# Sums over edges: strips cut by edges instead of by nodes, and a matmul that takes a node tile out of them

## The chip, the cores and the metric

One core of one Trainium2 chip runs the kernel. The metric is the device time in microseconds of one execution, as the median of several runs. One further execution was recorded by the hardware profiler; everything said of engines and waits comes from that one.

## The reference

The input is a matrix x of 6250 nodes by 512 features and a list of 100,000 edges (src, dst), sorted by dst; all is f32. With LN(v) = (v - mean) / sqrt(variance + 1e-5) over a row:

```
h0 = LN(x)
for layer in 1, 2:
    agg[n] = sum of h[src] over the edges whose dst is n
    deg[n] = number of those edges
    h = relu(h @ W_self + (agg / max(deg, 1)) @ W_neigh + b)
x = x + h
f = LN(x)
per node: the two of 8 experts with the largest f @ Wg, weights by softmax
    y_e = LN(relu(f @ W1[e] + b1[e]) @ W2[e] + b2[e]) * gamma[e] + beta[e]
x = x + weighted sum of the two y_e
```

All weight matrices are 512 by 512, except Wg (512 by 8).

## The kernel before

A **node tile** is 128 nodes: 49 of them. An **edge tile** is 128 edges: the rows h[src] of its edges, 128 by 512 f32 (256 KB), are fetched from memory by one indirect load on the POOL queue (a **gather**, L272). They are summed by dst on TensorE: a one-hot matrix `hot` (edges by nodes) is the stationary operand and the gathered rows the moving one, so that the output row of a node is the sum of its edges' rows.

The program has five stretches.

*Norms and edge tables.* x comes in twelve loads (`xt`) on the SP queue, is normed, turned, and written to `xn_d` in memory; the gathers of layer 1 read `xn_d`. For the first 19 node tiles (NS) the product with W_self of layer 1 is made here already and kept in `big` (`part(b)`); for the others the turned rows are kept there. Between the second and the third `xt` load, `edge_tables` makes two tables in the on-chip buffer: `srcT`, the indices of each gather, and `rel`, the dst of each edge relative to its group. A **group** is 256 nodes (25 groups). Since the edges of a group begin at any edge, a chain of operations counts the edges below each group (last edges of blocks of 1000, a comparison, a matmul, an indirect load, a comparison, a sum), and 50 loads on the SP queue then start at offsets read from registers.

*Layer 1* (`sums` with `layer1`). Each group is taken as having T = 34 edge tiles (15 in the last), more than it needs on average, so that nearly any draw fits: 831 gathers. A group's nodes are cut into eight **strips** of 32 nodes. Which edge tiles a strip can touch is not known when the program is built, so a span wide enough by 4.5 standard deviations is used: an edge tile is multiplied with every strip that it might touch (1.8 on average, 1513 strip matmuls per layer). A strip matmul has a stationary operand of 128 by 32 and occupies one of four column quarters of the array (`tile_position`); the quarters of 128 nodes fill the 128 partitions of one accumulator bank, `pa0` or `pa1` (one bank each). The order of edge tiles in a group alternates between its two ends, so that neighbours in the order fall into different quarters.

The order on TensorE, VectorE, ScalarE and POOL is written out by hand (`manual_schedule`): a loop over **slots** of four edge tiles. In slot i the program issues the gathers of slot i+2 into a ring of 12 row buffers, builds the `hot` matrices that fall due, adds two edge tiles, does the items due in the place "mid", adds two more, calls `finish` for a node tile whose last strip is complete, and does the items due in the place "post". `finish` for layer 1 (`layer1`) makes the degree from a sum of the hot matrices (`hs`, L292, `few`, L448, and a matmul `pn`, L449), scales the sum into `a` on ScalarE, and leaves items for the next slots: u0 (product of the own rows with W_self, only from tile 19 on, which opens an accumulator `pm`), u1 (turn `a`, L241 and L243), u2 (product with W_neigh, added to u0's accumulator, and one add, L427), u3 (turn), u4 and u5 (products with the two matrices of layer 2, written to memory as `z2` and `s2`). All products are in `project` (L413), four matmuls each; `pm` has three banks.

A check between the layers compares the sum of all degrees with the number of edges; where they differ, an unlimited but slow loop over all edges (`slow_path`) runs at the end.

*Layer 2* (`sums` with `route`). The neighbour product was applied before the sum, so the gathers read `z2`. `route` adds, norms, and chooses the experts of a tile over the next slots (`turn`, `logits`, `experts`, `rank`, two `send` on the POOL queue that scatter the rows into `xs` by expert, `share`, and at six points `take`, which makes the table of expert tiles known so far). In every second slot in which the table holds one, an **up-projection** (`Up`: load, turn, product `ph` at L734, turn, store) of an expert tile runs between the sums; there are 68 of them. Rows go through a ring of 12 parts of `big`. The last sends each wait for the send before.

*Experts.* 105 expert tiles are finished (the rest of the up-projections, the down-projections at L995, norm, store), the eight scatters of zero rows at the experts' ends each waiting for the one before, and the results are gathered per node and added.

Of the kernel before, what the change touches and what calls it, by code (L numbers as in the profile page):

```python
# [29 lines left out]
F32 = mybir.dt.float32  # L30
# [9 lines left out]
P = 128  # L40
SW = 32
NQ = P // SW
GN = 2 * P
# [4 lines left out]
RW = 1000  # L48
# [7 lines left out]
class Group:  # L56


    def __init__(self, g, N, E):
        self.g = g  # L60
        self.nodes = min(GN, N - g * GN)
        per = E / N
        self.T = ceil((self.nodes * per + 4 * sqrt(self.nodes * per)) / P)
        ns = ceil(self.nodes / SW)
        self.span = []
        for q in range(ns):
            a, z = q * SW * per, min((q + 1) * SW, self.nodes) * per
            lo = max(0, floor((a - 4.5 * sqrt(a)) / P))
            hi = min(self.T - 1, floor((z + 4.5 * sqrt(z)) / P))
            self.span.append((lo, self.T - 1 if q == ns - 1 else hi))  # L70
        self.nt = ceil(self.nodes / P)

        self.order = []
        cut = (self.T * P // GN) - 1 if self.nt == 2 else self.T
        for a, z in ((0, cut), (cut, self.T)):
            h = (z - a + 1) // 2
            for i in range(h):
                self.order += [t for t in (a + i, a + h + i) if t < z]
        self.strips = {t: [q for q, (lo, hi) in enumerate(self.span) if lo <= t <= hi] for t in self.order}
        self.first = {q: next(t for t in self.order if q in self.strips[t]) for q in range(ns)}  # L80
        self.last = {q: [t for t in self.order if q in self.strips[t]][-1] for q in range(ns)}

        self.done = [max(self.order.index(self.last[q]) for q in range(ns) if q // NQ == k)
                     for k in range(self.nt)]
        self.ns = ns
# [3 lines left out]
def gnn_moe(ctx, tc, x, src, dst, Ws1, Wn1, gb1, Ws2, Wn2, gb2, Wg, W1, b1, W2, b2, gamma, beta, out):  # L89
# [10 lines left out]
    groups = [Group(g, N, E) for g in range((N + GN - 1) // GN)]  # L100
    NG = len(groups)
    T = groups[0].T
    GB = P // T
    col = [g.g * T for g in groups]
    NCOL = col[-1] + groups[-1].T
    EP = E + T * P
    assert D == 512 and H == 512 and NE == 8 and E % RW == 0 and E // RW <= P

# [4 lines left out]
    dpad = dram.tile([EP], I32, name="dpad")  # L113
    spad = dram.tile([EP], I32, name="spad")

# [10 lines left out]
    iota_row = iota([P, GN], "iota_row", [[1, GN]])  # L126
# [14 lines left out]
    rel = edges.tile([P, NCOL], F32, name="rel")  # L141
    srcT = edges.tile([P, NCOL], I32, name="srcT")


    def edge_tables():
        with tc.tile_pool(name="prep", bufs=1, side="right") as prep, \
                tc.tile_pool(name="prep_r", bufs=3, side="right") as raw, \
                tc.tile_pool(name="prep_ps", bufs=1, space=PSUM) as pps:
            nrow = E // RW
            dst_r = dst.rearrange("(r e) -> r e", e=RW)  # L150
            last_i = prep.tile([nrow, 1], I32, name="last_i")
            nc.scalar.dma_start(last_i, dst_r[:, RW - 1 : RW])
            pad = prep.tile([T, P], I32, name="pad")
            nc.gpsimd.memset(pad, -1)
            pad0 = prep.tile([T, P], I32, name="pad0")
            nc.gpsimd.memset(pad0, 0)
            nc.scalar.dma_start(dpad[:E], dst)
            nc.scalar.dma_start(dpad[E:].rearrange("(t e) -> t e", e=P), pad)
            nc.scalar.dma_start(spad[:E], src)
            nc.scalar.dma_start(spad[E:].rearrange("(t e) -> t e", e=P), pad0)  # L160
            last = prep.tile([nrow, 1], F32, name="last")
            nc.vector.tensor_copy(last, last_i)
            thr = prep.tile([P, NG], F32, name="thr")
            nc.vector.tensor_scalar(thr, iota_row[:, :NG], float(GN), None, op0=OP.mult)
            thr_p = prep.tile([P, 1], F32, name="thr_p")
            nc.vector.tensor_scalar(thr_p, iota_p, float(GN), None, op0=OP.mult)
            below = prep.tile([nrow, NG], F32, name="below")
            nc.vector.tensor_scalar(below, thr[:nrow], last, None, op0=OP.is_gt)
            pr = pps.tile([NG, NDEG], F32, name="pr")
            nc.tensor.matmul(pr, below, ones[:nrow, :NDEG], start=True, stop=True)  # L170
            row = prep.tile([NG, 1], F32, name="row")
            nc.vector.tensor_scalar(row, pr[:, 0:1], float(nrow - 1), None, op0=OP.min)
            row_i = prep.tile([NG, 1], I32, name="row_i")
            nc.vector.tensor_copy(row_i, row)
            at_i = prep.tile([NG, RW], I32, name="at_i")
            nc.gpsimd.indirect_dma_start(
                out=at_i, out_offset=None, in_=dst_r,
                in_offset=bass.IndirectOffsetOnAxis(ap=row_i[:, 0:1], axis=0))
            at = prep.tile([NG, RW], F32, name="at")
            nc.vector.tensor_copy(at, at_i)  # L180
            nc.vector.tensor_scalar(at, at, thr_p[:NG], None, op0=OP.is_lt)
            cnt = prep.tile([NG, 1], F32, name="cnt")
            nc.vector.tensor_reduce(cnt, at, AX.X, OP.add)
            start = prep.tile([NG, 1], F32, name="start")
            nc.vector.scalar_tensor_tensor(start, row, float(RW), cnt, op0=OP.mult, op1=OP.add)
            ps = pps.tile([1, NG], F32, name="ps")
            nc.tensor.matmul(ps, start, ident[:NG, :NG], start=True, stop=True)
            starts = prep.tile([1, NG], I32, name="starts")
            nc.vector.tensor_copy(starts, ps)


            gbase = prep.tile([P, 1], F32, name="gbase")
            nc.vector.memset(gbase, 0.0)
            for k in range(1, GB):
                behind = prep.tile([P, 1], F32, name="behind")
                nc.vector.tensor_scalar(behind, iota_p, float(k * T), None, op0=OP.is_ge)
                nc.vector.scalar_tensor_tensor(gbase, behind, float(GN), gbase, op0=OP.mult, op1=OP.add)

            for k0 in range(0, NG, GB):
                gs = groups[k0 : k0 + GB]  # L200
                m = col[gs[-1].g] + gs[-1].T - col[k0]
                both = []
                for name in ("d", "s"):
                    both.append(raw.tile([P, P], I32, name=f"raw_{name}"))
                for g in gs:
                    o = nc.values_load(
                        starts[0:1, g.g : g.g + 1], engines=[mybir.EngineType.SP], min_val=0, max_val=E,
                        skip_runtime_bounds_check_because="a count of edges")
                    p0 = col[g.g] - col[k0]
                    for t, pad_d in zip(both, (dpad, spad)):  # L210
                        nc.sync.dma_start(t[p0 : p0 + g.T],
                                          pad_d[bass.ds(o, g.T * P)].rearrange("(t e) -> t e", e=P))
                cs = slice(col[k0], col[k0] + m)
                fd = raw.tile([P, P], F32, name="fd")
                nc.vector.tensor_scalar(fd[:m], both[0][:m], gbase[:m], float(k0 * GN),
                                        op0=OP.subtract, op1=OP.subtract)
                pd = pps.tile([P, P], F32, name="pd", bufs=2)
                nc.tensor.transpose(pd[:, :m], fd[:m], ident[:m, :m])
                nc.vector.tensor_copy(rel[:, cs], pd[:, :m])
                fs = raw.tile([P, P], F32, name="fs")  # L220
                nc.vector.tensor_copy(fs[:m], both[1][:m])
                pq = pps.tile([P, P], F32, name="pd", bufs=2)
                nc.tensor.transpose(pq[:, :m], fs[:m], ident[:m, :m])
                nc.vector.tensor_copy(srcT[:, cs], pq[:, :m])
# [12 lines left out]
    def transposed(pool, psp, t, func, n=P, out=None, bufs=2):  # L237

        pt = psp.tile([P, C, P], F32, name="pt")
        for c in range(C):  # L240
            nc.tensor.transpose(pt[:, c, :n], t[:n, c * P : (c + 1) * P], ident[:n, :n])  # L241
        tT = pool.tile([P, C, P], F32, name="tT", bufs=bufs) if out is None else out
        nc.scalar.activation(tT[:, :, :n], pt[:, :, :n], func)  # L243
        return tT


    def sums(z, pool, psp, count, finish, ring, nhot, each=None):

        slots = [(g, g.order[i : i + 4]) for g in groups for i in range(0, g.T, 4)]
        head = {}
# [970 lines left out]
```

## Time and profile before

| what | value |
|---|---|
| median of 3 runs | 3605.3 us (3600.63 to 3608.15) |
| profiled execution: time | 3591.62 us |
| profiled execution: span | 3589.7 us |
| busy: PE, VectorE, ScalarE, POOL | 82%, 33%, 16%, 53% |
| mean DMA rate | 202 GB/s |
| software queue (gathers, scatters) | 489 MB, 46% of 16 engines' span |
| last `xn_d` lands; first gather of layer 1 | 140.5 us; 141.4 us |
| `a` of tile 0, 19, 48 in layer 1 | 183.2, 686.1, 1443.1 us |
| layer-2 norm of tile 0, 17, 48 | 1518.1, 1977.8, 2889.8 us |
| experts | about 2970 us to the end |

The page of the profile gives times in microseconds unless marked ns. PE is TensorE's matmuls, PEld its weight loads (beside them), DVE VectorE, ACT ScalarE, POOL GpSimd, SP the engine that only issues loads and stores. The slices cut the span into 40 equal parts; a digit is the busy share in tenths (9 is 90% or more), and PEclk is TensorE's granted clock in tenths. A row of a group names line, engine, operation, output<-input, shape and count, then busy time and the mean of one in ns, then the idle time before these instructions and what ended most of it ("issue" is time in which the engine waited for nothing that is shown; "remote" is something outside the engines' own instructions). A row for a window gives its length, then busy time and count of PE, PEld, DVE, ACT and POOL, the clock, the DMA share and GB/s. An f32 matmul leaves two records.

### The profile page before, as it was taken

To read this page: it belongs to the slowest core of one execution; us is meant where nothing else is said; L and a number is where in the kernel's file an instruction comes from. 1 tells how busy PE (TensorE), PEld (TensorE's weight loads), DVE (VectorE), ACT (ScalarE), POOL (GpSimd) and SP (SyncE) were. 2 spreads that over 40 slices of the span, in tenths; PEclk is the share of its full clock that TensorE was granted. 3 is DMA by queue.
4 is the path that set the end of the run, shared out by engine and by line. 5 is a ranking of instruction groups with operands and counts; after the bars stand their busy time and mean duration, and the time that the engine had idled before them with its cause. 6 is when DMAs were issued, how large, how long until landed. Compare 5 with 4: busy or idle time off the path is not lost.

```text
span 3589.7 us, 37549 instructions
## 1 busy us (share of the span) xinstructions
PE 2948.7 (82%) x11789; PEld 1064.0 (30%) x11789; DVE 1182.7 (33%) x3728; ACT 586.8 (16%) x1058; POOL 1892.3 (53%) x2051
## 2 busy tenths in 40 slices
PE   7788888999999999555565788788878868999994
PEld 3222222333333333111111223233323323334442
DVE  5412212212222221122323333433343335443465
ACT  1200000101000010011111222222222212222221
POOL 0266556666666665366666656666566647000253
PEclk9899999999999999777777888999899989999997
DMA  5766666666666665576766777777777735441497
GB/s 195 240 184 202 195 195 202 203 198 197 205 200 188 193 197 173 205 216 206 216 213 212 232 228 232 224 242 228 225 237 241 236 112 171 133 130 59 163 311 237
DMA packets 277597, 724.86 MB, mean 202 GB/s; under 512 B 44079, under 2 KB 45889, under 8 KB 277234
## 3 DMA queue, kind: packets, MB, share of 16 engines
q0 software_dynamic: 150816, 489.21, 46.0%
q1 hardware_dynamic: 123160, 225.45, 18.5%
q10 hardware_dynamic: 3418, 7.73, 0.6%
q8 instruction: 99, 1.62, 0.2%
q14 instruction: 104, 0.85, 0.1%
HBM read 583.27 MB, written 139.74 MB: 201 GB/s over the span
## 4 chain that ended last, share of the span: by engine, by line
PE 69%; another core or an unknown queue 11%; issue 8%; DMA 4%; DVE 4%; ACT 3%; POOL 1%; SPq 0%; ACTq 0%; DVEq 0%; POOLq 0%
PE pa L301 21%; PE pm L413 17%; PE py L995 10%; PE ph L734 7%; PE pt L241 4%; PE ph L971 3%; PE pm L393 1%; PE ph L842 1%; PE small L801 1%; DMA xt<-in_x 1%; PE pt L742 1%; PE py L997 1%; ACT tT L243 1%; DVE st L229 0%
## 5 line engine op out<-in xcount | busy, mean ns | idle before, releaser
L272 POOL DMA_INDIRECT rows_t<-xn_d,srcT x831 | 789.3, 950 | 620.0 <-issue 202.1
L272 POOL DMA_INDIRECT big<-z,srcT x831 | 797.8, 960 | 524.9 <-issue 167.3
L301 PE MATMUL pa<-big,hot 128*32 128x512 f32 x3026 | 550.6, 681 | 9.6 <-issue 5.3
L301 PE MATMUL pa<-rows_t,hot 128*32 128x512 f32 x3026 | 478.7, 606 | 19.3 <-DVE hot L282 12.6
L413 PE MATMUL pm<-wn,tT 128*128 128x512 f32 x784 | 394.7, 650 | 101.1 <-ACT tT L243 65.1
L995 PE MATMUL py<-w,hT 128*128 x840 | 395.6, 614 | 41.6 <-DVE y L1012 21.1
L734 PE MATMUL ph<-big,xgT 128*128 x544 | 286.5, 676 | 98.1 <-ACT xgT L243 58.6
L931 POOL DMA_INDIRECT big<-ys,yrow x98 | 106.8, 1090 | 409.3 <-DMA ys<-y 314.6
L413 PEld LDWEIGHTS pm<-wn,tT 128*128 128x128 f32 x784 | 152.7, 205 | 345.1 <-issue 223.8
L995 PEld LDWEIGHTS py<-w,hT 128*128 128x128 f32 x840 | 153.6, 193 | 220.9 <-issue 176.3
L734 PEld LDWEIGHTS ph<-big,xgT 128*128 128x128 f32 x544 | 110.7, 214 | 262.1 <-issue 180.8
L243 ACT ACTIVATE tT<-pt 128x512 f32<-128x512 f32 x117 | 68.9, 596 | 726.6 <-PE pt L241 343.6
L413 PE MATMUL pm<-ws,tT 128*128 128x512 f32 x392 | 180.7, 604 | 0.0
L301 PEld LDWEIGHTS pa<-rows_t,hot 128*32 128x32 f32 x3026 | 89.5, 109 | 290.1 <-issue 233.2
L282 DVE TENSOR_TENSOR hot<-rel,iota_row 128x256 f32<-128x256 f32 (+3 forms) x392 | 155.6, 408 | 28.9 <-PE pa L301 12.3
L301 PEld LDWEIGHTS pa<-big,hot 128*32 128x32 f32 x3026 | 99.1, 116 | 196.0 <-issue 159.2
L971 PE MATMUL ph<-big,xgT 128*128 x296 | 136.9, 605 | 0.0
L847 POOL DMA_INDIRECT xs<-big,slot x98 | 99.3, 1013 | 69.4 <-issue 28.7
L427 DVE TENSOR_TENSOR h<-pm,bb 128x512 f32<-128x512 f32 x30 | 20.8, 692 | 339.6 <-PE pm L413 183.5
L1002 DVE BATCH_NORM_STATS2 st<-py 128x6 f32<-128x512 f32 x105 | 73.3, 698 | 153.6 <-PE py L997 151.2
L843 DVE TENSOR_TENSOR xa<-xa,ph 128x512 f32<-128x512 f32 (+1 forms) x49 | 33.7, 687 | 273.4 <-remote 144.4
L443 DVE TENSOR_TENSOR s<-pm,bb 128x512 f32<-128x512 f32 x49 | 33.9, 691 | 260.8 <-PE pm L413 201.9
(232 smaller groups left out, 2743.4 us busy)
## 6 DMA issues: line engine op xcount, KB each, us to landing
xg<-xs SPq DMA_DIRECT2D x105, 256.0 KB
ys<-y SPq DMA_DIRECT2D x105, 256.0 KB
hd<-hT SPq DMA_DIRECT2D x68, 256.0 KB
hT<-hd SPq DMA_DIRECT2D x68, 256.0 KB
rows_t<-xn_d,srcT POOLq DMA_INDIRECT x831
big<-z,srcT POOLq DMA_INDIRECT x831
xt<-in_x SPq DMA_DIRECT2D x12, 1024.0 KB
xn_d<-xn SPq DMA_DIRECT2D x12, 1024.0 KB
```

What stands on the lines that cost most here:

```text
L241: nc.tensor.transpose(pt[:, c, :n], t[:n, c * P : (c + 1) * P], ident[:n, :n])
L243: nc.scalar.activation(tT[:, :, :n], pt[:, :, :n], func)
L272: nc.gpsimd.indirect_dma_start(out=row, out_offset=None, in_=z[:, :], in_offset=bass.IndirectOffsetOnAxis(ap=srcT[:, c : c + 1], axis=0))
L282: nc.vector.tensor_tensor(hot[:, :m], rel[:, c0 : c0 + m].rearrange("p (t o) -> p t o", o=1).to_broadcast([P, m, SW]), iota_row[:, q * SW ...
L301: nc.tensor.matmul(pas[g.g, k][c : c + SW], hots[g.g, q][:, t - g.span[q][0]], gathered[g.g, t], start=(t == g.first[q]), stop=(t == g.las ...
L413: nc.tensor.matmul(ph, tT[:, c], w[:, c], start=(start and c == 0), stop=(stop and c == C - 1))
L734: nc.tensor.matmul(ph, self.xT[:, c], w1[:, bass.ds(self.e * KD + c * D, D)], start=(c == 0), stop=(c == C - 1))
L847: inst = nc.gpsimd.indirect_dma_start(out=xs[:, :], out_offset=bass.IndirectOffsetOnAxis(ap=slot[:n, b, k : k + 1], axis=0), in_=t["xn"][: ...
L931: nc.gpsimd.indirect_dma_start(out=yk[:n], out_offset=None, in_=ys[: ready[0] * P, :], in_offset=bass.IndirectOffsetOnAxis(ap=yrow[:n, b, ...
L971: nc.tensor.matmul(ph, u.xT[:, c], w1[:, bass.ds(u.e * KD + c * D, D)], start=(c == 0), stop=(c == C - 1))
L995: nc.tensor.matmul(py, hT[:, c], w2[:, bass.ds(e * KD + c * D, D)], start=(c == 0), stop=False)
L1002: nc.vector.bn_stats(st, py)
```

## The change

The strips are cut by edges. `Group` is gone. A strip is three consecutive edge tiles (`TS = 3`, 384 edges) and covers the 32 nodes that begin with the dst of its first edge; `rel` is the dst minus that. With the edge list cut at fixed places, the tables need no counts: 14 plain loads on the ScalarE queue, turns, and one broadcast of the strips' first dst. There are 782 edge tiles, 261 strips and 66 **rounds** of four strips, one strip to each quarter of an accumulator `pa` (two banks). A slot adds one edge tile to each of the four strips; three slots make a round, 197 slots a layer.

At a round's end ScalarE copies `pa` into `st_` (and, in layer 1, a matmul makes the degrees of the round's 128 rows, `counts`). Which rounds a node tile can have edges in is again taken with 4.5 standard deviations (`reach`, two to four rounds, 153 pairs over 49 tiles). When the last of them is closed, VectorE builds a 128 by 128 selection `sel` per round in "mid" of the next slot, and in "post" of it TensorE sums sel x st_ over the rounds into `ps` (and sel x counts in layer 1): `take_out`. Then `finish` runs as before.

In layer 1 the ring has 16 row buffers and gathers go three slots ahead; in layer 2 it stays at 12 and two. `pm` has two banks; u0 is a product of its own with its own add into `part(b)`, and u2's add always reads `part(b)`. In layer 2 `ps` is a buffer of `ph`. The last sends and the end scatters no longer wait for the ones before; a one-element memset on POOL (`apart`) stands between them. `yrow` moves to a later pool.

The core of the diff:

```diff
-    T = groups[0].T
...
+    NT_E = (E + P - 1) // P
+    NCH = (NT_E + TS - 1) // TS
+    NG = (NCH + NQ - 1) // NQ
+    reach = [rounds_of(b, N, E, NG - 1) for b in range(NB)]
+    most = max(z - a + 1 for a, z in reach)
...
     def edge_tables():
-            nc.gpsimd.indirect_dma_start(
-                out=at_i, out_offset=None, in_=dst_r,
-                in_offset=bass.IndirectOffsetOnAxis(ap=row_i[:, 0:1], axis=0))
...
-                        nc.sync.dma_start(t[p0 : p0 + g.T],
-                                          pad_d[bass.ds(o, g.T * P)].rearrange("(t e) -> t e", e=P))
...
+                    nc.scalar.dma_start(t[:full], e[k0 * P : (k0 + full) * P].rearrange("(t e) -> t e", e=P))
...
+        def close(i):
+            g = i // TS
+            k = len(tiles[i]) * SW
+            st = pool.tile([P, D], F32, name="st_", bufs=most)
+            nc.scalar.copy(st[:k], pa[0][:k])
+            strips[g] = st, k
+            pa[0] = None
+            if pn is not None:
+                nc.tensor.matmul(pn[:k, 0], few[g].rearrange("p q m -> p (q m)")[:, :k], ones_h[:, :NDEG],
+                                 start=True, stop=True)
+                counts[g] = pool.tile([P, NDEG], F32, name="counts", bufs=most + 1)
+                nc.vector.tensor_copy(counts[g][:k], pn[:k, 0])
+            for b in range(NB):
+                if reach[b][1] == g:
+                    at(i + 1, "mid", lambda b=b: prepare(b))
+                    at(i + 1, "post", lambda b=b: take_out(i + 1, b))
...
+        def take_out(i, b):
+            a, z = reach[b]
+            ps = room()
+            for g in range(a, z + 1):
+                st, k = strips[g]
+                sel = sels.pop((b, g))
+                nc.tensor.matmul(ps, sel[:k], st[:k], start=(g == a), stop=(g == z))
+                if pn is not None:
+                    nc.tensor.matmul(pn[:, 1], sel[:k], counts[g][:k], start=(g == a), stop=(g == z))
...
-            gather(i + 2)
+            gather(i + ahead)
...
             def u0():
-                own["ph"] = psp.tile([P, D], F32, name="pm", bufs=3)
-                project(own["ph"], xnT[b], ws1, True, False)
+                ps = psp.tile([P, D], F32, name="pm")
+                project(ps, xnT[b], ws1, True, True)
+                nc.vector.tensor_add(part(b), ps, bb1)
...
-                 lambda: pool.tile([P, D], F32, name="rows_t", bufs=12), 10)
+                 lambda: pool.tile([P, D], F32, name="rows_t", bufs=16), 16)
...
             def send(k):
+                if b >= NB - 4:
+                    apart()
...
-                free_of(inst, "xs", [sent[0]] if sent and b >= NB - 2 else ())
+                free_of(inst, "xs")
```

## The prediction

> **What bounds the kernel now.** I read the slices first, then the busy time of each engine by stage, then the groups of two engines inside a stage. In the slices (each about 90 us, the digits are tenths):
>
> ```profile
> PE   7788888999999999555565788788878868999994
> POOL 0266556666666665366666656666566647000253
> PEclk9899999999999999777777888999899989999997
> DMA  5766666666666665576766777777777735441497
> ```
>
> Seven stretches show: the norms (slices 1-2), layer 1 with PE at 8, layer 1 with PE at 9, layer 2 with PE at 5, layer 2 with PE at 7-8, a dip, and the experts with PE at 9. The change touches the first five. The busy time by stage (the first number is the length, then PE, PEld, DVE, ACT, POOL, clock, DMA share) puts sizes to four of them:
>
> ```profile
> 180.00:630.00 450.00, 372.78 (x1568) 124.91 (x1564) 93.82 (x235) 41.34 (x67) 270.44 (x286) 0.93 0.66 195
> 720.00:1440.00 720.00, 692.12 (x2822) 234.10 (x2821) 150.07 (x374) 67.80 (x110) 435.36 (x459) 0.99 0.66 193
> 1530.00:1980.00 450.00, 270.41 (x1314) 74.26 (x1314) 142.19 (x576) 69.28 (x116) 301.23 (x313) 0.74 0.70 211
> 1980.00:2880.00 900.00, 729.62 (x3446) 263.29 (x3444) 332.12 (x1316) 198.75 (x342) 554.97 (x576) 0.92 0.75 232
> ```
>
> 720-1440 is bound by TensorE: busy 96%. The other three are bound by no engine alone: PE 83%, 60% and 81%, POOL 60-67%. The cadence of the node tiles, from when their scaled sum or its layer-2 counterpart appears, is 26.5 us in the first, 26.0 in the second (720 us hold 27.7 tiles), 27.0 and 29.4 in the layer-2 pair. What POOL waits for, in the same order without the second (group, busy, idle and its releasers):
>
> ```profile
> L272 POOL DMA_INDIRECT rows_t<-xn_d,srcT x313 | 296.9, 948 | 194.2 <-PE pa L301 68.8 <-issue 68.0 <-remote 36.6
> L272 POOL DMA_INDIRECT big<-z,srcT x281 | 269.8, 960 | 135.5 <-issue 55.0 <-remote 50.5 <-PE pa L301 17.0
> L272 POOL DMA_INDIRECT big<-z,srcT x514 | 493.6, 960 | 323.1 <-issue 104.6 <-PE pa L301 85.6 <-remote 73.9
> ```
>
> A gather costs 0.95 us and about 0.30 of issue behind it, 1.25 us back to back: 17 per tile are 21.3 us. The rest of the 26.5 is POOL waiting for a row buffer that a sum (L301) still holds, while PE waits for rows: a ring of 12 with 8 gathers ahead ties the two together. In the TensorE-bound stage PE does this:
>
> ```profile
> L301 PE MATMUL pa<-rows_t,hot 128*32 128x512 f32 x1686 | 257.7, 602 | 0.0
> L413 PE MATMUL pm<-wn,tT 128*128 128x512 f32 x448 | 217.4, 630 | 27.5 <-issue 16.7 <-ACT tT L243 10.8
> L413 PE MATMUL pm<-ws,big 128*128 128x512 f32 x221 | 102.2, 605 | 0.0
> L413 PE MATMUL pm<-ws,tT 128*128 128x512 f32 x216 | 99.6, 604 | 0.0
> L449 PE MATMUL pn<-ones_h,few 128*128 128x8 bf16 x27 | 4.9, 180 | 0.0
> ```
>
> An f32 matmul is two records. Over 27.7 tiles: sums 9.3 us, four projections 15.1 (3.8 each, 0.95 a matmul), two turns 1.3, counts 0.2.
>
> **What the skill says.** The Trainium skill, "TensorEngine Tiling (Array Packing)", Key Properties, says that tiles of the array work independently and that a change of tiling mode drains the array. The trace agrees: a run of two, three or four strip matmuls in different columns takes the same, 0.99 us to the next operation; 8 take 1.92. So a strip matmul has no price of its own; a **run** has. "TensorE: Matmul & The Clock Gate", Part 1, says that an idle PE falls to half its clock; 0.74 in 1530-1980 against 0.99 fits, and means that PE time there shrinks once PE is fed. "DMA: Bandwidth & Descriptors", Anatomy of one DMA, gives 2.0 us plus bytes/436e3, an estimate of 2.6 us for 256 KB; the trace has 3.3 us from a gather's issue to its landing, which I use.
>
> **The change, part by part.** One unit is the node tile; after the change it has 782/49 = 16.0 gathers and 197/49 = 4.02 slots (before 17.0 and 4.49).
>
> *Removed.* 49 gathers per layer, 1.25 us each on POOL: 1.25 us a tile. Strip matmuls fall from 1513 to 782 per layer, and each slot now has four in four different columns: one run of 0.99 us, two where a turn splits the slot (two of 4.02 in layer 1): 6.0 runs, 6.0 us, against 9.3: **-3.3 us a tile** of PE. DVE loses the 196 reductions (0.58 us); it is 21-37% busy, so nothing.
>
> *Added on PE.* 153 take-outs per layer (3.12 a tile): one 128x128 by 128x512 matmul at 0.95 us, 2.95 us a tile. In layer 1 also 153 count matmuls (same stationary, 8 columns, f32). No row has one. From below: a 128x128 f32 turn, 0.66/4 = 0.16; from above: half a take-out, 0.47. I take 0.30 (two weight loads, 0.2 us each, partly covered): 0.94 a tile. Round counts 1.35 x 0.18 against 0.18: +0.06. Sum **+0.6 us a tile in layer 1** (+0.2 to +1.2), about **+0.9 in layer 2**, where the sums save only 2.0 as more turns split the slots.
>
> *Added waits.* Each round's copy of pa (ACT, 66 per layer, 0.6 us) lets go one of two pa buffers and the take-out comes a whole slot (6 us) later; ACT is under 22% busy: nothing; if ACT were late, the next round's first sum and every projection behind it in PE's order would stand, at most 1 us a round or 66 us a layer. The three pm buffers become two; a pm is drained in 0.7 us while the next projection runs 3.8: nothing; uncovered, 0.7 per projection. u0's own add (30 on DVE, 0.69) is hidden the same way. In layer 2 the take-out shares ph with the up-projections and share(): its two scalar_tensor_tensor reads, 1.4 us, let it go; nothing while another ph is free, 1.4 a tile if not.
>
> *Moved: the ring.* Layer 1 gets 16 row buffers and gathers three slots ahead. POOL's wait for pa, 68.8 us over 490 (18.5 tiles), is 3.7 a tile. Layer 2 keeps 12 and two ahead.
>
> *Edge tables.* The chain of counts, an indirect load and 50 loads on SP, 0.72 us each, which held SP from 27 to 64 us ahead of the third xt load, becomes 14 loads on ACT's queue. The stage ends when the last xn_d lands, at 140.5; xn_d was queued behind these loads too. DMA is busy 0.64 there and later loads still follow: of 37 us I count **-7** (-25 to +8, as the loads of the next weights stand behind them on ACT).
>
> *Sum, against the profiled execution.*
> - Norms: -7.
> - Layer 1, tiles 0-18: PE 372.8/17.0 = 21.9 a tile, +0.6 = 22.5; POOL 16 x 1.25 = 20.0. PE bounds if rows come in time; I leave it 2.0 of its 4.6 us of idle: 24.5 against 26.5, x19 = **-38** (-75 to +11, the latter if the ring brings nothing).
> - Layer 1, the other 30: +0.6 x 30 = +18, less part of the 1.0 us of idle a tile, which the deeper ring fills: **+10** (-15 to +40).
> - Layer 2, first 18: POOL's pace, 450/313 = 1.44 us an operation with both sends; one operation less is -1.4 a tile, of which PE at a clock of 0.74 gives back 0.2: -1.2 x 18 = **-22** (-60 to +15).
> - Layer 2, the other 31: -1.25 on POOL, +0.9 on PE, each idle a good share of the time: net -0.5 x 31 = **-15** (-60 to +40).
> - Up-projections: one every second slot, 68 of them, start at slot 80 of 220 before; all fit. With 197 slots, from 74 and with two halts for the next table, six remain after the last gather. One is 270.7/64 + 1.4 = 5.6 us: 34 us, of which the earlier tail had about half: **+15** (0 to +35).
> - Experts: the eight end scatters and last sends no longer wait for each other, mostly beside PE work: **-3** (-15 to 0).
>
> Together -60. The profiled execution took 3591.6 us (span 3589.7), 13.7 under the median; taken off the median of 3605.3 this gives **3545 us**.
>
> **Rivals.**
> - *The take-out costs more than the strips save (slower).* In layer 1 PE is the bound. If a full-array matmul between column-tiled runs pays the drain at each change of mode, the split runs take 1.05 and a count matmul 0.47, a tile has 6.3 + 3.12 x (1.06 + 0.47) + 0.24 = 11.3 against 9.5: +1.8 x 49 = +88 in layer 1, less 40 where the ring helps; layer 2 +1.2 x 31 = +37, tail +15, gathers -25, norms -7: about +68, 3673. It decides once sum and take-out together pass 9.5 us a tile by more than the idle that the ring removes, about 0.8 us over all 49. For it: PE at 96%; against it: the mode changes today too, at every turn, and 0.99 includes it.
> - *PE-neutral and the stalls stay (no change).* Tiles now come every three or every six slots instead of evenly, so PE has nothing but sums for three slots and POOL's 5 us a slot shows, then PE lags. The ring's gain goes into this, the rest cancels: -5 to +5, 3600-3610. For it: 17 of 49 gaps are of six slots; against it: 16 buffers span three slots of POOL's work.
> - *Both layers reach POOL's pace.* Layer 1 at 24 for 19 tiles (-48), layer 2 at 18 x 1.35 = 24.3 and 27.0: -49 and -74, layer 1's rest at 25.5 (-15), tail +15: -170, 3435. For it: PE's clock would rise when fed; against it: PE then needs 24 in layer 2 at full clock, 95% of the time.
> - That the strips don't fit, and the slow loop over all edges runs, would add milliseconds; with 16 edges a node 384 edges cover some 24 of 32 nodes. Under 1 in 100.
>
> **Chances and range.** About 0.2% (7 us) is what a measurement of this kernel can tell from no change. The forecast's case (3490 to 3597) 0.45, POOL's pace 0.12, no change 0.08, the take-out's case with its milder forms 0.35. Faster 0.57, same 0.08, slower 0.35. The range 3455 to 3665 leaves out some 1 in 10 on each side; the likeliest case alone is 3490 to 3597.
>
> **What would show it.** Right: POOL's wait for pa in 180-630 under 1 us a tile, tiles there at 24-25 us; sums 6.0 us a tile in 720-1440, take-out and counts 3.9, tiles at 26-27; layer 2 at 25-26 and 28-29; norms ended near 133. Wrong: a take-out over 1.1 us or a count over 0.5; PE waiting for st or sel; POOL's wait for pa in layer 2 above 3 us a tile; over ten up-projections after the last gather.

## The result and the profile after

The changed kernel takes **3661.4 us** (median of 4, 3658.6 to 3665.7) against 3606.7 for the kernel before: a ratio of 1.0146 (95% interval 1.0112 to 1.0180). It is slower by about 55 us, where 60 us less was forecast. The profiled execution took 3665.66 us, its span is 3663.9, 74.2 over the profiled span of before.

The slices of the page:

```profile
PE   7778888999999999466666888888888877999994
POOL 0266555555555552466666555555555438000253
PEclk9889999999999999777777888898898988999997
DMA  6566666665666653666666766666677634441496
```

In layer 1 POOL is at 5 where it was at 6: the gathers, 98 fewer in both layers, show. PE is at 9 as before in most of layer 1. The dip between the layers is a little deeper (4), most slices of layer 2 are a tenth higher (6 where they were 5, 8 where some were 7), and the two slices before the experts are at 7, where they were 6 and 8. What POOL and PE do (rows of the page):

```profile
PE 3038.6 (83%) x9794; PEld 1156.2 (32%) x9794; DVE 1131.4 (31%) x4001; ACT 659.3 (18%) x1188; POOL 1800.4 (49%) x1970
L214 POOL DMA_INDIRECT rows_t<-xn_d,srcT x782 | 742.1, 949 | 654.9 <-PE pa L244 262.9
L214 POOL DMA_INDIRECT big<-z,srcT x782 | 752.6, 962 | 609.3 <-issue 167.9
L244 PE MATMUL pa<-big,hot 128*32 128x512 f32 x1564 | 443.9, 684 | 107.5 <-DVE hot L224 63.0
L244 PE MATMUL pa<-rows_t,hot 128*32 128x512 f32 x1564 | 348.5, 632 | 93.1 <-DVE hot L224 30.0
```

POOL is 92 us less busy than before (1892.3), PE 90 us busier (2948.7), though it has 1995 fewer instructions. The 92 us less gathering bought nothing: POOL's wait for the sums in layer 1 grew from 193 to 263 us. PE is now idle for 201 us ahead of the strip sums, 93 of it ended by a `hot`; before, it was idle there for 29 us. PE's busy time by line, each instant counted once, shows where its 90 us come from: sums 974 to 742, take-outs (L278) 0 to 323, count matmuls (L280) 0 to 19, all else -19.

In the TensorE-bound stretch of layer 1, 720 to 1440 us, the PE groups of the changed kernel are:

```profile
L386 PE MATMUL pm<-wn,tT 128*128 128x512 f32 x432 | 202.9, 613 | 8.2 <-ACT tT L190 7.9 <-issue 0.3
L244 PE MATMUL pa<-rows_t,hot 128*32 128x512 f32 x851 | 177.8, 622 | 23.5 <-DVE deg L419 17.1 <-DVE rcnt L421 3.3 <-DVE rcnt L420 3.2
L386 PE MATMUL pm<-ws,tT 128*128 128x512 f32 x218 | 100.9, 605 | 0.0
L386 PE MATMUL pm<-ws,big 128*128 128x512 f32 x216 | 97.9, 596 | 0.0
L280 PE MATMUL pn<-counts,sel 128*128 128x8 f32 x172 | 24.5, 214 | 0.0
```

`pm<-wn,tT` holds two projections a tile, of eight records each, so 432 records are 27 tiles: sums 6.6 us a tile (6.0 was worked out), counts 0.91 (0.94). The view puts the waits of the sums to `deg` and `rcnt`: VectorE stands at the degree of a finished tile, and the next `hot`, which the program builds one slot ahead, is queued behind it (in one of these waits the degree starts at 778.46 us, after 10.9 us of waiting, the `hot` ends at 779.19, and the sum starts at 779.24).

Cutting both spans at the same events gives this account (us):

| stretch | before | after | difference |
|---|---|---|---|
| start to first gather of layer 1 | 141.4 | 148.1 | +6.7 |
| first gather to `a` of tile 0 | 41.8 | 62.2 | +20.4 |
| `a` of tile 0 to `a` of tile 48 | 1259.9 | 1243.2 | -16.7 |
| from there to the sum of tile 0 in layer 2 | 75.0 | 94.6 | +19.6 |
| tile 0 to tile 48 in layer 2 | 1371.7 | 1383.6 | +11.9 |
| from there to the end | 699.9 | 732.2 | +32.3 |

The steady stretches together gain 5 us; the four ends cost 79.

### The profile page after: what moved, and what is told of

Same layout as the page of the kernel before. It is cut to its first block, busy times and chain, and to the rows that moved or that the text cites. A ratio compares the mean times of both kernels' runs of the same rounds, so it can differ in the third digit from the quotient of the medians.

```text
span 3663.9 us, 33902 instructions
## 1 busy us (share of the span) xinstructions
PE 3038.6 (83%) x9794; PEld 1156.2 (32%) x9794; DVE 1131.4 (31%) x4001; ACT 659.3 (18%) x1188; POOL 1800.4 (49%) x1970
## 4 chain that ended last, share of the span: by engine, by line
PE 70%; another core or an unknown queue 10%; DVE 7%; issue 6%; DMA 4%; ACT 2%; SPq 0%; DVEq 0%; POOL 0%; ACTq 0%; POOLq 0%
PE pm L386 17%; PE pa L244 15%; PE py L969 9%; PE ph L709 7%; PE ph L278 5%; PE pt L188 4%; PE ph L945 3%; PE ps L278 2%; PE ph L816 2%; PE pm L366 2%; DMA out<-acc 1%; PE small L775 1%; DMA xt<-in_x 1%; PE pt L717 1%
## 5 line engine op out<-in xcount | busy, mean ns | idle before, releaser
L214 POOL DMA_INDIRECT rows_t<-xn_d,srcT x782 | 742.1, 949 | 654.9 <-PE pa L244 262.9
L214 POOL DMA_INDIRECT big<-z,srcT x782 | 752.6, 962 | 609.3 <-issue 167.9
L244 PE MATMUL pa<-big,hot 128*32 128x512 f32 x1564 | 443.9, 684 | 107.5 <-DVE hot L224 63.0
L244 PE MATMUL pa<-rows_t,hot 128*32 128x512 f32 x1564 | 348.5, 632 | 93.1 <-DVE hot L224 30.0
L386 PE MATMUL pm<-wn,tT 128*128 128x512 f32 x784 | 368.6, 613 | 22.0 <-ACT tT L190 21.7
L386 PEld LDWEIGHTS pm<-wn,tT 128*128 128x128 f32 x784 | 144.9, 195 | 207.8 <-issue 163.7
L244 PEld LDWEIGHTS pa<-big,hot 128*32 128x32 f32 x1564 | 65.9, 114 | 247.9 <-issue 111.7
L720 DVE TENSOR_SCALAR hT<-pt,b1T 128x128 f32<-128x128 f32 x272 | 76.6, 344 | 166.4 <-PE pt L717 132.3
L244 PEld LDWEIGHTS pa<-rows_t,hot 128*32 128x32 f32 x1564 | 47.4, 110 | 233.5 <-issue 130.8
L224 DVE TENSOR_TENSOR hot<-rel,iota_row 128x128 f32<-128x128 bf16 (+1 forms) x394 | 106.0, 281 | 26.6 <-issue 12.4
```

The lines of the kernel that those rows point to most:

```text
L214: nc.gpsimd.indirect_dma_start(out=gathered[t], out_offset=None, in_=z[:, :], in_offset=bass.IndirectOffsetOnAxis(ap=srcT[:, t : t + 1], a ...
L224: nc.vector.tensor_tensor(hots[i][:, :m], rel.rearrange("p (c j) -> p j c", j=TS)[:, j, g * NQ : g * NQ + m] .rearrange("p (t o) -> p t o" ...
L244: nc.tensor.matmul(pa[0][q * SW : (q + 1) * SW], hots[i][:, q], gathered.pop(t), start=(j == 0), stop=(j == TS - 1 or t == NT_E - 1), tile ...
L386: nc.tensor.matmul(ph, tT[:, c], w[:, c], start=(start and c == 0), stop=(stop and c == C - 1))
L720: nc.vector.tensor_scalar(hT[:, c], pt[:, c], b1T[:, bass.ds(self.e * HC + c, 1)], 0.0, op0=OP.add, op1=OP.max)
```

## The experiments

Each time is set against the kernel before on the same chip. The chips of the first two groups of experiments (e1 to e8; "the quicker chip" below) ran the kernel before in 3229 and 3230 us; those of the later ones (e9 to e14) took 3600 and 3642 for it. The changed kernel's ratio on the quicker chip agrees with that of the first comparison (e5), so ratios are compared throughout. What is said of waits and tiles comes from one profile of each kernel.

**e1, hots three slots ahead.**

```diff
-            hots[i] = pool.tile([P, NQ, SW], F32, name="hot", bufs=4)
+            hots[i] = pool.tile([P, NQ, SW], F32, name="hot", bufs=6 if pn is not None else 5)
...
-            build(i + 1)
+            build(i + 3)
```

> The changed kernel with the one-hot matrices built three slots ahead instead of one (5 or 6 hot buffers, 2 few buffers). Theory A, late hots: the PE idle in front of the strip sums that ends with a DVE hot or a DVE instruction ahead of it (200 us over both layers in the changed kernel against 29 before) is what ate the gain of the fewer gathers; it falls below 60 us, and the time falls by 40 to 120 us, to 3540-3620. Theory B, the take-outs' own work on PE: idle moves to another name and the time stays within 15 us of 3661.

3252.7 us, ratio 1.0073 (1.0049 to 1.0096); the changed kernel has 1.0152 (e5), so 26 us are won. What PE waited for longest, in the changed kernel on this chip and then in e1 (us in total, times, longest):

```profile
PE pa L244 <- DVE hot L224: 83.8, 33, 8.4
PE pa L244 <- DMA big<-z,srcT: 35.8, 55, 4.1
```

```profile
PE pa L244 <- DMA big<-z,srcT: 69.0, 94, 4.2
PE py L970 <- DVE y L987: 23.0, 1, 23.0
```

The wait for `hot` is gone, 84 us, and 33 of it come back as waits for gathers. The gain is in the second part of layer 2: 24.06 us a tile became 23.37 over 31 tiles, 21 us. In layer 1 it is nothing (24.52 to 24.49 in its last 29 tiles). Theory A holds for about half of the loss, less than its range said.

**e4, the kernel before with late hots.** `max(0, need - 5 + min(q, 4))` became `max(0, need - 1)`.

> The kernel before with its hot matrices built one slot ahead of their first use instead of up to five. Theory A: PE idle in front of the sums rises from 29 us to over 100 us and the time by 30 to 100 us. Rival: the idle only takes the place of waits for gathers, and the time stays within 10 us of 3605.

3228.6 us, ratio 0.9998 (0.9987 to 1.0009): nothing. Built one slot ahead, a `hot` is hardly ever late here: PE waits 18 us for them in all, 13 of it once, where it waits 84 in the changed kernel. In the changed kernel one `hot` serves every sum of a slot, while before a slot needs a new one only when a strip begins; that this is the reason was not tested by itself. Since its time is that of the kernel before, this run stands for it in the windows below.

**e5, the changed kernel again, as the anchor.**

> The changed kernel again, as the anchor for the other kernels of this group, since the chip of the experiments ran the kernel before in 3229 us instead of 3606. Where the PE work decides (theory B): the ratio to the kernel before stays 1.010 to 1.018 on any chip. Where late hots decide (theory A): a chip on which PE's releases come promptly has less of it, and the ratio is under 1.008, no more than that of the kernel with early hots (1.007).

3278.5 us, ratio 1.0152 (1.0135 to 1.0169). It is the ratio of the first comparison, on a chip that is 10% quicker, as theory B expected. The windows of the same six stretches as above, for e4 (as the kernel before) and then for e5 (length, then PE, PEld, DVE, ACT, POOL, clock, DMA share, GB/s):

```profile
0.00:140.80 140.80, 101.25 (x370) 53.72 (x370) 85.06 (x273) 40.08 (x99) 3.17 (x13) 0.93 0.64 229
140.80:170.70 29.90, 22.59 (x79) 3.34 (x79) 7.07 (x18) 0.00 (x0) 22.90 (x24) 0.85 0.68 194
170.70:1294.20 1123.50, 1121.70 (x4760) 377.43 (x4759) 267.42 (x663) 118.47 (x192) 768.85 (x808) 1.00 0.73 219
1294.20:1361.50 67.30, 33.63 (x120) 13.15 (x118) 10.07 (x32) 2.47 (x4) 22.91 (x24) 0.75 0.58 206
1361.50:2520.00 1158.50, 1017.09 (x4862) 325.33 (x4863) 479.95 (x1927) 269.48 (x466) 868.42 (x902) 0.99 0.83 268
2520.00:3225.00 705.00, 610.12 (x1602) 259.60 (x1600) 324.44 (x818) 153.58 (x298) 208.45 (x283) 0.93 0.50 164
```

```profile
0.00:148.60 148.60, 107.76 (x364) 56.77 (x364) 81.82 (x258) 39.86 (x99) 2.17 (x13) 0.90 0.62 215
148.60:190.40 41.80, 32.81 (x71) 5.74 (x72) 3.37 (x17) 1.17 (x2) 31.75 (x34) 0.91 0.70 199
190.40:1317.20 1126.80, 1124.16 (x3926) 431.31 (x3922) 224.57 (x798) 154.54 (x255) 710.48 (x749) 1.00 0.68 205
1317.20:1400.80 83.60, 46.96 (x123) 14.45 (x127) 10.65 (x36) 4.70 (x8) 32.65 (x35) 0.80 0.63 226
1400.80:2541.30 1140.50, 994.50 (x3642) 340.78 (x3640) 482.52 (x2038) 298.39 (x518) 814.79 (x847) 0.96 0.81 255
2541.30:3275.00 733.70, 634.10 (x1676) 272.00 (x1676) 333.14 (x858) 158.45 (x307) 209.60 (x294) 0.94 0.49 160
```

This is the plainest view of the case. The third rows are layer 1: by the record PE is busy for all but 2 to 3 us of some 1125, before and after, from the first tile on. There the change is worth about what it does to PE's work: +2.5 us of busy time, +3.3 of length, in 48 tiles. Layer 2 (fifth rows) gains 18 us. The ends lose: +7.8 (norms), +11.9 and +16.3 (first tile of each layer), and +28.7 (last sum to the end).

**e6, fewer take-outs.** `4.5 * sqrt(...)` in `rounds_of` became `3.0 * sqrt(...)`.

> The changed kernel with reach drawn at 3.0 standard deviations instead of 4.5: 130 take-outs per layer instead of 153, at most three a tile; everything else stays. Theory B, the take-outs' own work on PE: 46 take-outs at 1.05 us and 23 count matmuls at 0.3 us are 55 us less PE work, of which 35 to 55 us show: 35-55 us under the unchanged changed kernel. Theory A (late hots), or theory D (the wait for whole rounds at both ends of a layer): under 15 us.

This leaves out 23 of the 153 take-outs of each layer. 3246.4 us, ratio 1.0057 (1.0037 to 1.0077): 32 us under e5. PE's busy time in the page of e6:

```profile
PE 2886.9 (89%) x9656; PEld 1096.7 (34%) x9656; DVE 1126.2 (35%) x3955; ACT 657.8 (20%) x1188; POOL 1799.5 (56%) x1970
```

Against 2940.3 in e5 it is 53 us less, 55 were worked out, and 60% of it shows; PE's waits for a `hot` grow from 84 to 104 us. Theory B holds, a little under its range.

**e7, no count matmuls.** The matmul into `pn[:, 1]` is left out of `take_out`. With it go the true degrees (a constant 16 stands for them) and the comparison of their sum with the number of edges.

> The changed kernel without the 153 count matmuls of the take-out; the degree is set to a constant 16, so the neighbour means are not those of the reference. Theory B: 153 x 0.14 to 0.3 us, 20 to 45 us less in layer 1, where PE is the bound: 15-40 us under the changed kernel. Rival: they are hidden beside weight loads and the time stays within 8 us.

3253.8 us, ratio 1.0063 (1.0046 to 1.0081): 25 us less. 153 count matmuls cost 0.16 us each, about the price of a turn's transpose, the lower of the two bounds.

**e8, the old ring.** `bufs=16), 16)` became `bufs=12), 12)`, and with it gathers go two slots ahead.

> The changed kernel with the old ring of 12 row buffers and two slots ahead in layer 1. The prediction gave the deeper ring 38 us or more in layer 1. If that holds, 25-60 us slower than the changed kernel, all of it in the gathers' stretch of layer 1; if PE is the bound there (theory B), within 10 us, because POOL then only waits longer for PE.

3286.6 us, ratio 1.0171 (1.0154 to 1.0188), 8 us over e5, with overlapping intervals. **e11, the kernel before with the new ring:** its layer 1 gathers three slots ahead into 16 buffers (and has one `hot` buffer less).

> The kernel before with the ring of 16 row buffers and three slots ahead in layer 1 (one hot buffer less). The prediction's step gave a deeper ring 2 us a tile in tiles 0-18: 38 us. If TensorE bounds these tiles too, as the chip of the experiments shows (PE busy 1122 of 1124 us in layer 1), within 8 us of the kernel before.

3609.7 us, ratio 1.0028 (1.0011 to 1.0045): nothing gained, and this on a chip about as slow as that of the prediction's profile, where POOL's waits had looked recoverable. Its tiles 0 to 18 take 27.1 us each, against 26.5 in that profile. The depth of the ring was worth nothing alone, and with the strips no more than 8 us (0.2%), which the intervals do not set apart from nothing.

**e2, up-projections in two of three slots,** and **e3, this with e1's hots.** `if i % 2 or ...` became `if i % 3 == 2 or ...`.

> The changed kernel with an up-projection allowed in two slots of three instead of one of two. Theory C, tail: the ten up-projections that ran after the last gather, about 7.5 us each in slots that are otherwise nearly empty, are the reason for the 32 to 49 us by which the stretch from the last gather to the end grew; four or fewer are left there, that stretch falls by 35-50 us, and the sums' stretch of layer 2 grows by no more than 20: the time falls by 20-45 us. Rival: PE is the bound in layer 2, the up-projections lengthen its stretch by what the tail loses, and the time stays within 10 us.

> Both: hots three slots ahead and up-projections in two slots of three. Theories A and C together: the two gains add, 60 to 160 us under the changed kernel, 3500-3600, at or under the kernel before. Rival: with hots early, layer 2 becomes PE-bound and the tail's gain is lost: no better than the hots alone.

e2: 3270.9 us, ratio 1.0131 (1.0109 to 1.0152). e3: 3267.5, ratio 1.0124 (1.0104 to 1.0143), which is 15 us *slower* than e1. In e3 five up-projections and more than half of a sixth follow the last gather instead of ten, and the first down-projection comes 73.9 us after it instead of 95.8; but the last gather is at 2529.6 instead of 2486.6. What the tail loses, the sums' stretch gains and more. In e2 the tail loses 22 us and the last gather comes 15 later than in e5. Theory C falls, but for 8 us at most: the longer tail is mostly PE work that moved there, not a cost of its own.

**e9, early hots and fewer take-outs.** The edits of e1 and e6.

> Early hots (three slots ahead) and 130 take-outs per layer together, in the changed kernel. If the two costs are separate (late hots in layer 2, PE work in both layers), their gains of 26 and 32 us add to 50-60 us: 3218-3228 where the changed kernel takes 3278, at or a little under the kernel before (3230). If narrower take-outs only filled PE time that waited for late hots, or the other way round, under 40 us together: 3238 or more, slower than before.

3604.3 us, ratio 1.0002 (0.9979 to 1.0026), where the changed kernel has 1.015. Alone they were worth 0.8% and 0.95%; together they give about 1.5%, so they add in full or for the greater part, which the interval leaves open. The result is level with the kernel before.

**e10, take-out in the closing slot.** `at(i + 1, "mid", ...)` and `at(i + 1, "post", ...)` in `close` became `at(i, "post", ...)`.

> The changed kernel with sel built and the take-out made in the slot that closes the round, not one slot later. Theory D (both ends of a layer wait for whole rounds): the first tile of each layer and the last come 4-6 us earlier, 10-20 us in all, less what PE waits for the copy of pa and for sel, at most 1.5 us x 98: the time lies between 15 us faster and 60 us slower, and the trace shows PE idle before L278. If the slot's distance were idle weight, it would be faster by 10 or more.

3685.5 us, ratio 1.0236 (1.0194 to 1.0277), 0.9% slower than the changed kernel. The first tile of each layer does come 4.8 and 4.3 us earlier, by one profile each, but PE now waits for `sel`, which the slot's distance had covered (waits of PE in e10; in the changed kernel all waits of L278 for `sel` are 4.8 us):

```profile
PE ph L278 <- DVE sel L269: 46.0, 21, 10.9
...
PE ps L278 <- DVE sel L269: 22.4, 4, 18.9
```

The distance of a slot is worth keeping. **e12, the weights' loads on the SP queue.** `wn1`, `wn2` and `ws2` are loaded from the SP queue; in the program their loads stand after the last `xn_d` store.

> The changed kernel with the three weight loads of layer 1 (3 MB) put behind the last xn_d store on the SP queue, instead of at 25-38 us on ACT's. The first gather of layer 1 starts at 148 in the changed kernel and at 141 before. If these loads ahead of the x loads cost the 7 us, the first gather starts at 140-143 and the time falls by 0-7 us (the loads then stand beside the first gathers); if the stage is set by PE's work alone, nothing moves.

3654.9 us, ratio 1.0145 (1.0101 to 1.0190). The loads did not become late: SP issues them at 13.7, 20.4 and 25.3 us, ahead of the fourth load of x, where the changed kernel issues them from ACT's queue at 24.8, 30.4 and 34.6. So the run does not test what it was made for. The first gather starts at 139.6 instead of 148.1: where these loads stand among the others bears on the end of the norms, and why stays open. The time does not tell it from nothing.

**e13, counts in bf16.** `counts` is bf16, VectorE makes a bf16 copy of `sel`, and the count matmul uses both.

> The changed kernel with the count matmul in bf16 (counts and a bf16 copy of sel made on DVE; whole numbers up to 256 are exact). If the price of the counts is that f32 takes two weight loads and two passes, at least half of what leaving them out saved (25 us of 3278, 0.75%) is saved: a ratio to the kernel before of 1.007 to 1.012 where the changed kernel has 1.015. If it is the break between two take-outs, 1.013 or more.

3680.6 us against 3641.9, ratio 1.0109 (1.0073 to 1.0145): 0.4% better than the changed kernel's 1.015, about half of the 0.9% that leaving the counts out gives; the interval reaches to both answers. **e14, all of it:** the edits of e1, e6, e12 and e13.

> Early hots, 130 take-outs, bf16 counts and the late weight loads together. If the costs found are all that the strips add (steady stretches), the ratio to the kernel before is 0.990 to 0.997, the first version that is faster than both; the ends (first tile of each layer and the last gather to the experts) still cost 30 to 60 us more than before. If something else grows with them, 0.998 or more.

3619.2 us against 3641.9, ratio **0.9939** (0.9911 to 0.9967): faster than both kernels. The loads of e12 go out early here too (13.7 to 24.8 us). Its profile has 24.7 and 25.7 us a tile in the two parts of layer 1 (25.65 and 26.06 in the changed kernel), but the ends are as late as expected: 61.8 us from the first gather to tile 0, 94.6 between the layers, ten up-projections after the last gather.

## Why the prediction was wrong

It forecast -60 us; it was +55, and +74 between the two profiles, which is 134 from the forecast. Two steps failed. The prediction let the gathers set the pace of a tile wherever neither engine was busy throughout, and so counted a saved gather and a deeper ring as gain: tiles 0 to 18 of layer 1 and both parts of layer 2, together -75, measured -4. And it put the later first tile of each layer at nothing: measured +40. The tail (20), the norms (14) and the rest of layer 1 (11 the other way) make up the difference. Step by step:

- **Tiles 0-18 of layer 1, the largest term (-38; measured -15.6): the step that failed.** It took 4.6 us of PE idle a tile as PE waiting for rows, which a deeper ring would bring. PE did not wait for rows. In the whole profile of before, the sums wait 4 us for gathered rows; the idle time of 230 to 630 us stands at the product with W_neigh, which waits for the turn on ScalarE (rows of before: sums of layers 2 and 1, then the product in 230:630):

```profile
L301 PE MATMUL pa<-big,hot 128*32 128x512 f32 x3026 | 550.6, 681 | 9.6 <-issue 5.3 <-DMA big<-z,srcT 2.0 <-DVE hot L282 1.2
L301 PE MATMUL pa<-rows_t,hot 128*32 128x512 f32 x3026 | 478.7, 606 | 19.3 <-DVE hot L282 12.6 <-issue 4.1 <-DMA rows_t<-xn_d,srcT 2.0
L413 PE MATMUL pm<-wn,tT 128*128 128x512 f32 x233 | 127.5, 697 | 63.4 <-ACT tT L243 47.8 <-issue 15.6
```

  In the changed kernel this wait is smaller, and one for `hot` stands in its place (the same 400 us):

```profile
L386 PE MATMUL pm<-wn,tT 128*128 128x512 f32 x245 | 114.0, 608 | 11.0 <-ACT tT L190 11.0
L244 PE MATMUL pa<-rows_t,hot 128*32 128x512 f32 x512 | 108.1, 636 | 44.4 <-DVE hot L224 30.0 <-DVE rcnt L420 7.9 <-issue 6.5
```

  POOL's wait for `pa`, which was to fall under 1 us a tile, is 58.1 us in these 15.6 tiles, 3.7 as before. e11 shows on a chip like this one that the ring brings nothing, and e4 and e5 show hardly a gap in PE's record in these tiles on the quicker one. Why the turn came late can be followed in one case of before. From its timeline, ScalarE and then POOL (start, us, engine, line, operation, in brackets the idle time before):

```profile
287.61 0.69 ACT L454 ACTIVATE a<-pa,rcnt 128x512 f32<-128x512 f32 x1 [6.54 <-PE pn L449]
299.33 0.60 ACT L243 ACTIVATE tT<-pt 128x512 f32<-128x512 f32 x1 [11.03 <-remote]
```

```profile
296.65 0.94 POOL L272 DMA_INDIRECT rows_t<-xn_d,srcT  x1 [0.48 <-remote]
298.08 0.94 POOL L272 DMA_INDIRECT rows_t<-xn_d,srcT  x1 [0.49 <-remote]
```

  The four transposes that this turn waits for are recorded as ended at 290.2, PE as idle from 291.3 to 300.0. Yet the releases of seven PE instructions with recorded ends from 287.9 to 290.2 came at 290.7, 292.1, 293.5, 295.0, 296.4, 297.8 and 299.25 us, one every 1.43 us; the last is that of the transposes, and ScalarE starts right after it. The Trainium skill, "Perfetto Trace Analysis", Tensor Engine Instruction (MATMUL, LD_WEIGHTS), says that a matmul's end in a profile is computed, and that its release goes out when the accumulator has acknowledged the writes. The trace fits the first, with 9 us between the recorded end and the reader's start here; what the releases waited for it does not show. The granted clock is 1.00 from 285 to 295 us and 0.50 from 295 to 302. So it stays open whether PE was still working in that time or stood still behind its own late releases; either way it did not lack rows. Why releases come so late on this chip and not on the quicker one, no run here tells.
- **PE's own terms** were about right in size. Sums 6.6 us a tile against 6.0, take-outs 323/306 = 1.05 us on this chip and 285/306 = 0.93 on the quicker one against 0.95; for a count, 0.16 us by e7 against 0.30. (A run of eight strip matmuls takes 1.85 us to the next operation; the 1.92 is the length of its own record. Nothing hangs on it.) Summed over both layers the forecast was +74 us; PE's busy time grew by 90, and by 34 on the quicker chip. The rest of layer 1, forecast at +10, is -1.1.
- **The first tile of each layer was put at nothing, without a reason.** The prediction has the take-out come a slot later and asks only whether ScalarE is late. But the first sum of a layer needs two whole rounds, 24 gathers, a copy and a slot, where 19 gathers were enough before. When it is ready, POOL has issued 34 gathers in layer 1 and 35 in layer 2, where it had issued 24 (second and fourth rows of the windows above); on the first chip 45 and 40 against 30 and 28. At 1.25 us a gather these 10 to 15 more are an estimate of 13 to 19 us. Measured: +20.4 and +19.6, on the quicker chip +11.9 and +16.3. That is 40 of the 74 us between the two profiles, and 28 of 50 on the quicker chip. e10 takes out the slot and brings 4.8 and 4.3 of it back; the rest was not tested by a run.
- **Layer 2** (-22 and -15; measured +7.5 and +4.4): the same failed step. One gather less a tile was to be passed on whole, on a chip where the sums of layer 2 waited 2 us for rows. On the quicker chip they wait 99 us for rows in e4 and 36 in e5, and there the layer does get shorter, by 8.5 and 9.6 us; early hots (e1) bring 21 more in the second part: a wait that the prediction had not listed took part of the place of the gather. It named "PE waiting for st or sel" as a sign of failure, not `hot`, though the step from up to five slots ahead (one for half of the strips) to one for all was in the diff.
- **Up-projections** (+15; measured +32 with what follows): ten ran after the last gather, not six. e2 and e3 show that it is mostly an exchange with the sums' stretch.
- **Norms** (-7; measured +6.7): the weights' loads went out at 24.8 to 34.6 us, where they had gone out at 67.6 to 74.5, a risk that the prediction named. That this is what held the norms up is not shown (e12). **Experts** (-3): first down-projection to end 661.5 before, 665.0 after; nothing.

The first rival (take-outs cost more than strips save, 3673) was nearest in number, and right that PE's work counts: e6 and e7 take 32 and 25 us off. It placed most of the loss in the steady tiles of layer 1, which are level on the quicker chip and 17 us shorter on the first; most of the loss is at the ends.

## What to carry to other kernels

Before idle time of an engine is counted as a gain, look which of its instructions the idle time stands in front of, and what ended it: POOL waiting for a sum and PE being idle in the same stretch do not yet mean that PE waits for POOL. Where waits are called "remote", or releases come long after the recorded ends, the busy share of that engine says little of how much room it has. A pipeline that hands on results in larger pieces pays at the start of every pass; count the first piece in the sum, separately from the cadence. When a slot comes to need one operand for all its work, see how far ahead that operand is built: here VectorE, whose order is fixed by hand, stood at the work of a finished tile, and the next slot stood with it (early hots, e1, are worth 26 us).

## What the runs showed of the hardware

The kernel before took 3229 and 3230 us on two chips, and 3600, 3607 and 3642 on others. PE's recorded busy time is nearly the same (2906 us in e4, 2949 in the kernel before). What differs is when its releases arrive: of 3047 PE instructions that release others the slower trace has 2524 separate releases, and 247 intervals of 1.38 to 1.47 us between two of them, the quicker one (e4) 3099 of 3101 and 21 such intervals. The granted clock differs too: 0.91 against 0.97 over the run, 0.74 against 0.99 in the first part of layer 2. Which of these is cause and which effect, no run tells. Yet the change costs the same share on both, 1.46% and 1.52%.
